# Splitting projected pieces of q and k on VectorE and GpSimd, in a graph attention kernel on one core

## The chip, the core and the metric

The kernel runs on one core of a Trainium2 chip. A core has TensorE (PE, matrix products; PEld in the profile is its loading of weights), VectorE (DVE), ScalarE (ACT), GpSimd (POOL) and SyncE (SP, which here issues all DMAs). They run their own streams of instructions, each in order, and wait for one another by semaphores. The metric is the device time of one execution in microseconds (us); the time before is a median of three runs.

## What is computed

Two layers over N = 2708 nodes with D = 128 features and a dense matrix adj, 2708 x 2708. The first is an attention in which adj is added twice to the scores; almost all of the work is there.

```python
# layer 0
q = (x @ Wq.T).reshape(d, n, h)      # d = 128, n = 2708, h = 8
k = (x @ Wk.T).reshape(d, n, h)
v = (x @ Wv.T).reshape(d, n, h)
a = einsum('dnh,dmh->dnm', q, k) * d ** -0.5 + adj + adj
a = softmax(a, axis=2)
out = einsum('dnm,dmh->dnh', a, v).reshape(n, h * d) @ Wo.T
x = layernorm(x + out)
# layer 1: two products with adj, and a second layernorm
hid = adj @ (x @ W2) + b2
x = layernorm(x + adj @ (hid @ W4) + b4 + hid @ res_w.T + res_b)
```

The reshape makes 128 independent attentions ("d"), each over 2708 queries and 2708 keys with 8 numbers per query and key: 128 x 2708 x 2708, some 940 million exponentials.

## The kernel before

**Scores.** With q scaled by half of D ** -0.5, exp(2 (q k + adj)) is the weight. The 128 attentions go in 32 groups of four (GB), the queries in six blocks of 452 (QB; the last has 448), the keys in 21 chunks of 128 and a short one of 20. q and k are each kept as two float32r numbers, a rounded part and what is left over, so that a score is one product with 32 rows of q and k per attention, four attentions side by side in PE.

**Two ways to a weight.** For most chunks, DVE adds adj to two scores at a time (L417, from PSUM into a tile `e`), and ACT takes exp of up to eight at once (L512). For nine of the chunks (TWO_EXP), ACT takes exp of three bare scores (L509, from the PSUM tile `p` into a tile `w`) and POOL multiplies them by exp(2 adj) (L510). The tiles exp(2 adj), `ecol`, are made by ACT in group 0 (L398), stored to DRAM, and loaded from there in all later groups (L298). The weights are multiplied with v and summed up in PSUM by PE (`add_up`, L427 to L435). DVE copies the sums of a block out (`hand_on`, L441), and SP stores them (L443).

**Steps.** A block is nine steps, one for each chunk of TWO_EXP: two to four "pieces" (pairs of scores) that DVE adds, three scores for POOL, and one exponential of each kind. There are 32 x 6 x 9 = 1728 steps, 54 to a group. ACT's work in a step is L509 and then L512.

**The order on PE.** The function `interleave` plans ahead in what order PE gets scores ("piece"), sums ("add_up"), copies ("hand_on") and projections ("amid"). It keeps an account of times (`pe`, `act`, `pool`, and `added`, the times at which DVE's adds end) with constants such as PRODUCT (a sum over a chunk), PROJECT and SPLIT, and gives PE next what it expects to be ready. A score needs one of two PSUM buffers (tag `s`), which comes free when DVE has added from it; a projection takes one of the same buffers.

**Projections amid the loop.** The first 256 of x's rows are projected ahead of the loop, two chunks of 128 (FIRST) by three weights. They suffice for group 0. The other 20 chunks are projected within it, as 120 "pieces of projection" (`halves`: chunk, one of k, q and v, half of the 1024 columns), each a product of 128x128 by 128x512 (L349). Two v pieces follow four of k and q. The list `amid` gives the step ahead of which each stands. `project` gives the product to PE, and DVE takes it from PSUM. For a v piece that is one copy (L352). For a q or k piece `split` reads PSUM twice, for the rounded part (L330) and for what is left over (L331), and then reduces the rounded part to its largest magnitude in `ends` (L332). The store, two DMAs for a q or k piece (L358), is put off to the next step, after its second piece, and waits there on SP. `load_half` loads the weights for the next piece.

**Bounds.** After the first layer the kernel looks whether its exponentials stayed in a safe range, and runs a slower attention with maxima if not. The largest q and k in `ends` are part of that.

**Other work in a group's steps.** SP loads adj (L295, L302) and exp(2 adj) (L298) eight tiles ahead, the next group's keys in steps 0 to 31 and the next block's q. POOL orders the next group's keys (L261) in steps 33 to 49 and spreads its values (L278, L279) in steps 50 to 53.

Of the kernel before, what the change touches and what calls it, by code (L numbers as in the profile page):

```python
# [9 lines left out]
F32 = mybir.dt.float32  # L10
# [8 lines left out]
P = 128  # L19
H = 8  # L20
GB = 4
NB = 512
# [5 lines left out]
SUM_HIGH = 1e30  # L28


QK_LIMIT = 7.5
EPS = 1e-5


# [4 lines left out]
def interleave(plan, blocks, short, amid=(), bufs=4, patience=0.1):  # L39

    SCORES, SAME_ROWS, AFTER_SHORT, SHOWN, PRODUCT, SHORT_PRODUCT, AGAIN, ADD, OVERLAP, COPY, MULTIPLY, HOP = (
        0.40, 0.2, 0.31, 0.15, 0.89, 0.96, 0.80, 1.04, 0.03, 0.56, 3.1, 0.12)
    EXP, EXP_ADDED, EXP_TILE = 0.07, 0.14, 0.37
    PROJECT, SPLIT = 0.95, 1.75  # L50
    n_plan = len(plan)
    users = [{m for p in pieces for m, _ in p} | {two} for pieces, two, _ in plan]
    held = {}
    for i, (pieces, two, _) in enumerate(plan):
        for p in pieces:
            for m, _ in p:
                held.setdefault(m, set()).add((False, i))
        held.setdefault(two, set()).add((True, i))
    complete = [[m for m in sorted(held, key=lambda m: (m != short, m)) if max(i for _, i in held[m]) == k] for k in range(n_plan)]
    first_chunk, last_chunk = ends_of(plan, short)  # L60
    pe = act = pool = banks = free_acc = 0.0
    added = [-1.0, -1.0]
    ready, summed, queue, sums, again = {}, {}, [], None, False
    n, c, left = 0, 0, None
    amid, seen = set(amid), 0
    while n < blocks * n_plan or queue:
        starts = []
        if n in amid and c == 0 and seen < n:
            starts.append((added[-2] + HOP, "amid"))
        elif n < blocks * n_plan:  # L70
            (b, i), (ob, oi) = divmod(n, n_plan), divmod(n - bufs, n_plan)
            pieces, two, batches = plan[i]
            left = list(batches) if left is None else left
            tiles = pieces[c]
            old = [summed.get((ob, x)) for x in users[oi]] if n >= bufs else [0.0]
            if None not in old:
                at = added[-2] + HOP
                rows = [r for m, j in tiles for r in (range(GB) if m == short else [j])]
                beside = [j for j in left if j not in rows][:2] if banks + HOP <= max(pe, at) else []
                if c == len(pieces) - 1:  # L80
                    beside = list(left)
                    at = max(at, banks + HOP) if left else at
                starts.append((at, "piece"))
        if queue and not (queue[0][1] == first_chunk and sums is not None):
            qb, qm = queue[0]
            at = max([ready[p, qb * n_plan + k] for p, k in held[qm]] + [free_acc] * (qm == first_chunk)) + HOP
            starts.append((at, "add_up"))
        soon = [s for s in starts if s[0] <= pe + patience]
        at, what = soon[0] if soon else min(starts)
        pe = max(pe, at)  # L90
        if what == "add_up":
            queue.pop(0)
            pe += SHORT_PRODUCT if qm == short else AGAIN if again else PRODUCT
            again = True
            summed[qb, qm] = pe
            yield "add_up", qb, qm, None
            if qm == last_chunk:
                sums = qb, pe
            continue
        again = False  # L100
        if what == "amid":
            pe += PROJECT
            added.append(max(added[-1], pe + SHOWN) + SPLIT)
            seen = n
# [36 lines left out]
def graph_attention_gcn(ctx: ExitStack, tc: tile.TileContext, x, xT, adj, adjT, adjP, adjS,  # L141
# [39 lines left out]
    near_exp = {(b, m): dram.tile([P, QB], F32, name=f"ne{b}_{m}") for b in range(len(QBS)) for m in TWO_EXP}  # L181


    ends = const.tile([P, 2, 2 * NM], F32, name="ends")
    nc.gpsimd.memset(ends, 0.0)


    with ExitStack() as s:
# [135 lines left out]
            t = t.rearrange("p a b -> p (a b)")  # L324
            return t if n == 1 else t.rearrange("p (n w) -> p n w", n=n)

        def split(o, src, i, end, mul=nc.vector.tensor_scalar_mul):

            f = half_scale if i == 1 else 1.0
            mul(o[:, 0].bitcast(F32R), src, f)  # L330
            nc.vector.scalar_tensor_tensor(o[:, 1].bitcast(F32R), src, f, o[:, 0], ALU.mult, ALU.subtract)  # L331
            nc.vector.tensor_reduce(end, o[:, 0], AX.X, ALU.max, apply_absolute_value=True)  # L332

        def load_half(n):
            c, i, h = halves[n]
            i0, mi = MC[c]
# [6 lines left out]
        def project(n):  # L343

            c, i, h = halves[n]
            i0, mi = MC[c]
            dst = projections[i][1]
            pp = ps.tile([P, 2, NB], F32, tag="s", name="s")
            nc.tensor.matmul(pp[:mi, 0, :], given[c][:, :mi], given.pop((c, i, h)), start=True, stop=True)  # L349
            o = proj.tile([P, 2, NB], F32, tag="pr", name="pr")  # L350
            if i == 2:
                nc.vector.tensor_copy(o[:mi, 0], pp[:mi, 0])  # L352
                return lambda: nc.sync.dma_start(dst.rearrange("(i g) e -> i (g e)", g=P)[ds(i0, mi), ts(h, NB)], o[:mi, 0])
            split(o[:mi], pp[:mi, 0], i, ends[:mi, i, ds(2 * c + h, 1)])

            def store():
                for l in range(2):
                    nc.sync.dma_start(dst.rearrange("r (i g) -> i r g", g=P)[ds(i0, mi), ds(H * l + 4 * h, 4)],  # L358
                                      o[:mi, l].rearrange("p (e g) -> p e g", g=P))
            return store  # L360

        first_x = flat(ppool.tile([P, 3, QB], F32, tag="w", name="w"))
        nc.sync.dma_start(first_x[:, : FIRST * P], xT[:, : FIRST * P])
# [6 lines left out]
        for i, (_, dst) in enumerate(projections):  # L370
            for c in range(FIRST):
# [5 lines left out]
                    nc.scalar.copy(o[:, 0], flat(pp))  # L377
                    nc.sync.dma_start(dst.rearrange("(i g) e -> i (g e)", g=P)[ts(c, P)], o[:, 0])
                else:
                    split(o, flat(pp), i, ends[:, i, 2 * c : 2 * c + 1], nc.scalar.mul)  # L380
                    nc.sync.dma_start(dst.rearrange("r (i g) -> i r g", g=P)[ts(c, P)],
                                      o.rearrange("p l (e g) -> p (l e) g", g=P))
            if i == 1:
# [10 lines left out]
        def first_exp(b, m):  # L394

            nw = QBS[b][1]
            t = ecols.tile([P, QB], F32, tag="ecol", name="ecol")
            nc.scalar.activation(t[:, :nw], adj_cols[0, b, -1 - m][:, :nw], AF.Exp, scale=2.0)  # L398
            nc.sync.dma_start(near_exp[b, m][:, :nw], t[:, :nw])
            exp_cols[0, b, m] = t  # L400

        def score(to, g, b, m, j):
            nw = QBS[b][1]
# [40 lines left out]

        where = {}

        amid = list(range(2, 54, 6))
        amid += range(56, 56 + 13 * (len(halves) - len(amid)), 13)
        for g in range(1, NG):
            c = (min(NG, g + 2) * GB * N - 1) // (P * P)  # L450
            assert c < FIRST or amid[halves.index((c, 2, 1))] + 8 < 54 * g
        stores = []
        loaded = ahead
        for what, n, c, beside in interleave(plan, len(steps) // len(plan), NU, amid):
            if what == "amid":
                at = amid.index(n)
                stores.append(project(at))
                if at + 1 < len(halves):
                    load_half(at + 1)
                continue  # L460
# [7 lines left out]
            g, b, i = steps[n]  # L468
            pieces, two, _ = plan[i]
            nw = QBS[b][1]  # L470
            if c == 1 and stores:
                stores.pop()()
            if c == 0:
                nq = (g, b + 1) if b + 1 < len(QBS) else (g + 1, 0)
                if i == 3 and nq[0] < NG:
# [30 lines left out]
            add_near(e, st, g, b, pieces[c], at)  # L506
            at += 2
            if c == len(pieces) - 1:
                nc.scalar.activation(w[:, :, :nw], sp[:, :, :nw], AF.Exp, scale=2.0)  # L509
                nc.gpsimd.tensor_mul(w[:, :, :nw], w[:, :, :nw],  # L510
                                     exp_cols[g, b, two][:, :nw].unsqueeze(1).to_broadcast([P, 3, nw]))
# [42 lines left out]
    def layer0_out(sb, ps, pa, judge):  # L554
# [72 lines left out]
        if judge:  # L627
# [1 line left out]
            nc.vector.tensor_scalar(finite, ys.rearrange("p c f -> p (c f)"), 0.0, 0.0, ALU.mult, ALU.is_equal)  # L629
            nc.vector.tensor_reduce(fine[:, 0:1], finite, AX.X, ALU.min)  # L630
            bounds = [(reach[:, 0, :], ALU.min, SUM_LOW, ALU.is_ge), (reach[:, 1, :], ALU.max, SUM_HIGH, ALU.is_le)]
            for i in range(2):
                limit = QK_LIMIT * (1.0, half_scale)[i]
                bounds.append((ends[:, i, :], ALU.max, limit, ALU.is_le))
# [195 lines left out]
```

## Time and profile before

| | |
|---|---|
| median of three runs | 6994.23 us (6991.26 to 6994.96) |
| the profiled execution | 7000.04 us, its span 6998.3 us |
| ahead of the loop | to 46.9 us |
| the loop, 32 groups | from 46.9 us to some 6658 us |
| group 0 (nine pieces of projection) | 235.2 us |
| groups 1 to 27 (111 pieces, three to five in a group) | 202.6 to 209.0 us each |
| groups 28 to 30 (no piece; nor has 31) | 200.1 us each |
| the rest (out of the first layer, second layer) | some 340 us |

A group's time is read from the start of POOL's first multiplication (L510) in one group to that in the next.

The costliest groups of instructions, with the count, the time that they were busy and the mean of one:

| line, engine | what | count | busy us | mean ns |
|---|---|---|---|---|
| L510 POOL | w times exp(2 adj), 128x1356 | 1728 | 5349.2 | 3101 |
| L417 DVE | scores plus adj, 128x904 | 5568 | 5889.6 | 1092 |
| L512 ACT | exp of e | 1728 | 4625.9 | 2677 |
| L509 ACT | exp of p | 1728 | 2312.3 | 1338 |
| L349 PE | projection, 128x512 | 240 | 134.2 | 641 |
| L330, L331, L332 DVE | split of a q or k piece | 80 each | 55.3, 55.3, 54.0 | 691, 691, 675 |
| L352 DVE | copy of a v piece | 40 | 27.6 | 691 |

In the profile, "idle before, releaser" names the time that an engine stood still ahead of an instruction and whose work ended that. In a timeline each line has the start and the duration in us, the engine, the line of the kernel, the operation, what is written and read, the shapes, and in brackets the idle time ahead of it. A line of a table by windows has the window, its length, the busy time of PE, PEld, DVE, ACT and POOL (with the number of instructions), the granted clock of PE, the share of the DMA engines that was busy, and GB/s. The end of a matmul is modelled, so PE's busy share is not a measure of what PE has left.

### The profile page before, as it was taken

Reading aid. Unit: us, or ns where it says so; the run is one execution under the profiler, and the core shown is the slowest. Engines: PE = TensorE matmul, PEld = TensorE weight load, DVE = VectorE, ACT = ScalarE, POOL = GpSimd, SP = SyncE. Lnnn points to the kernel's source line nnn. Section 1 sums busy time; section 2 is a strip of 40 time slices with the busy share of each in tenths; the row PEclk is TensorE's granted clock in tenths of the full one; section 3 lists DMA queues with packets and bytes.
Section 4 is the critical chain, followed back from the end, with each engine's and each line's share of the span. In section 5 each row is a group of like instructions: output and inputs, shape, how many; then the busy total and the mean of one; then the engine's idle time right before and its main releaser. Section 6 shows DMA issues by size and latency. Waiting matters only on the chain.

```text
span 6998.3 us, 137155 instructions
## 1 busy us (share of the span) xinstructions
PE 6733.7 (96%) x50426; PEld 2044.4 (29%) x50426; DVE 6186.2 (88%) x6363; ACT 6509.2 (93%) x3605; POOL 5624.8 (80%) x2387
## 2 busy tenths in 40 slices
PE   7999999999999999999999999999999999999979
PEld 2222222222222222222222222222222222222254
DVE  7899999999999999999999999999999999999941
ACT  7999999999999999999999999999999999999920
POOL 5888888888888888888888888888888888888800
PEclk8999999999999999999999999999999999999999
DMA  8877777777787777877777777877777777777667
GB/s 276 266 243 241 238 240 238 241 237 243 242 247 238 238 239 236 249 237 239 239 235 244 241 248 242 241 237 238 246 238 241 233 234 239 235 230 229 222 195 234
DMA packets 1143256, 1674.14 MB, mean 239 GB/s; under 512 B 148922, under 2 KB 1090366, under 8 KB 1138478
## 3 DMA queue, kind: packets, MB, share of 16 engines
q1 hardware_dynamic: 1142574, 1665.29, 77.0%
q8 instruction: 399, 6.54, 0.4%
q14 instruction: 283, 2.32, 0.1%
HBM read 1582.90 MB, written 81.80 MB: 238 GB/s over the span
## 4 chain that ended last, share of the span: by engine, by line
PE 49%; DMA 14%; DVE 12%; issue 8%; ACT 7%; SPq 5%; POOL 5%; DVEq 0%; ACTq 0%; POOLq 0%
PE acc L435 23%; PE s L410 16%; DVE e L417 10%; DMA col<-in_adjP 6%; POOL w L510 5%; ACT w L509 3%; ACT e L512 3%; PE acc L657 3%; DMA two<-in_adjP 3%; SPq L286 3%; DMA ecol<-ne 2%; PE p L410 2%; PE acc L427 2%; PE acc L432 1%; PE s L349 1%
## 5 line engine op out<-in xcount | busy, mean ns | idle before, releaser
L510 POOL TENSOR_TENSOR w<-w,ecol 128x1356 f32<-128x1356 f32 (+1 forms) x1728 | 5349.2, 3101 | 991.1 <-ACT w L509 864.0
L417 DVE TENSOR_TENSOR e<-s,col 128x904 f32<-128x904 f32 (+1 forms) x4608 | 4840.8, 1092 | 394.6 <-PE s L410 217.7
L512 ACT ACTIVATE e<-e 128x2712 f32<-128x2712 f32 (+5 forms) x1728 | 4625.9, 2677 | 61.1 <-DVE e L417 60.2
L435 PE MATMUL acc<-e,vals 128*9 128x452 f32 x20352 | 3564.6, 547 | 0.5 <-ACT e L512 0.2
L410 PE MATMUL s<-q,k 32*128 32x452 f32 x10944 | 2488.0, 464 | 134.8 <-DVE e L417 71.2
L509 ACT ACTIVATE w<-p 128x1356 f32<-128x1356 f32 (+1 forms) x1728 | 2312.3, 1338 | 94.4 <-PE p L410 54.2
L410 PEld LDWEIGHTS s<-q,k 32*128 32x128 f32 x10944 | 1032.3, 183 | 3320.4 <-DVE e L417 2817.3
L435 PE MATMUL acc<-w,vals 128*9 128x452 f32 x10368 | 1634.3, 548 | 0.0
L410 PE MATMUL p<-q,k 32*128 32x452 f32 (+1 forms) x5184 | 1282.5, 444 | 21.9 <-ACT w L509 20.9
L417 DVE TENSOR_TENSOR e<-s,two 128x904 f32<-128x904 f32 (+1 forms) x960 | 1048.8, 1093 | 91.2 <-PE s L410 34.1
L435 PEld LDWEIGHTS acc<-e,vals 128*9 128x9 f32 x20352 | 457.1, 89 | 818.4 <-issue 794.5
L410 PEld LDWEIGHTS p<-q,k 32*128 32x128 f32 x5184 | 529.6, 183 | 70.5 <-ACT w L509 55.4
L435 PEld LDWEIGHTS acc<-w,vals 128*9 128x9 f32 x10368 | 207.6, 89 | 217.4 <-issue 184.4
L261 POOL CAST k<-k_raw 128x336 fp32r<-128x336 f32 x251 | 222.4, 887 | 34.3 <-DMA q<-qs 34.3
L432 PE MATMUL acc<-e,v_first 128*32 128x452 f32 (+1 forms) x1536 | 188.3, 559 | 52.5 <-DVE o L441 46.3
L427 PE MATMUL acc<-e,v_short 128*128 128x452 f32 (+1 forms) x384 | 196.8, 594 | 0.0
L349 PE MATMUL s<-wc,xc 128*128 128x512 f32 (+1 forms) x240 | 134.2, 641 | 0.0
L441 DVE COPY o<-acc 128x452 f32<-128x452 f32 x192 | 118.7, 618 | 6.2 <-PE acc L435 6.2
L657 PE MATMUL acc<-col,xw 128*128 128x512 f32 (+2 forms) x264 | 105.8, 550 | 0.0
L657 PE MATMUL acc<-col,hw 128*128 128x512 f32 (+2 forms) x264 | 104.1, 545 | 0.0
L549 ACT ACTIVATE sd<-mv,eps 128x1 f32<-128x1 f32 (+1 forms) x22 | 5.9, 291 | 104.7 <-DVE mv L543 104.7
L669 ACT COPY hw<-ph 128x128 f32<-128x128 f32 (+1 forms) x22 | 5.4, 265 | 98.7 <-PE ph L668 98.6
(86 smaller groups left out, 1044.0 us busy)
## 6 DMA issues: line engine op xcount, KB each, us to landing
col<-in_adjP SPq DMA_DIRECT2D x1965, 226.0 KB
two<-in_adjP SPq DMA_DIRECT2D x1440, 226.0 KB
ecol<-ne SPq DMA_DIRECT2D x1395, 226.0 KB
col<-in_adjP SPq DMA_DIRECT2D x393, 224.0 KB
two<-in_adjP SPq DMA_DIRECT2D x288, 224.0 KB
ecol<-ne SPq DMA_DIRECT2D x279, 224.0 KB
col<-in_adjT SPq DMA_DIRECT2D x210, 256.0 KB
k_raw<-ks SPq DMA_DIRECT2D x512, 84.6 KB
```

Source lines behind the costliest of these rows:

```text
L261: copy(k[:, :, ts(i, n)], t[:, ts(i, n * NU)].rearrange("p (q c) -> p c q", c=NU))
L286: nc.sync.dma_start(q[ds(32 * j + 2 * H * i, 2 * H), :nw].bitcast(F32), qs[:, ds((GB * g + j) * N + n0, nw)])
L349: nc.tensor.matmul(pp[:mi, 0, :], given[c][:, :mi], given.pop((c, i, h)), start=True, stop=True)
L410: nc.tensor.matmul(to[:, :nw], k[r, m, :], q[r], start=True, stop=True)
L417: nc.vector.tensor_add(e[:, ds(at, 2), :nw], st[:, :, :nw], a)
L427: nc.tensor.matmul(a[:, :nw], vz, e[:, t, :nw], start=False, stop=False)
L432: nc.tensor.matmul(a[ds(32 * j, 32), :nw], v_first[g % 2][:, ds(32 * j, 32)], e[:, t, :nw], start=True, stop=False)
L435: nc.tensor.matmul(a[ds(32 * j, VW), :nw], v[:, m, ds(VW * j, VW)], e[:, t, :nw], start=False, stop=(m == last_chunk))
L509: nc.scalar.activation(w[:, :, :nw], sp[:, :, :nw], AF.Exp, scale=2.0)
L510: nc.gpsimd.tensor_mul(w[:, :, :nw], w[:, :, :nw], exp_cols[g, b, two][:, :nw].unsqueeze(1).to_broadcast([P, 3, nw]))
L512: nc.scalar.activation(e[:, :at, :nw], e[:, :at, :nw], AF.Exp, scale=2.0)
L657: nc.tensor.matmul(acc[:, :nw], src[:mw, m, :], t[:mw, :nw], start=(m == 0), stop=(last is None and m == NM - 1))
```

## The change

Four things change.

- `project`: DVE takes a q or k piece from PSUM in one pass, scaled, into a tile `pa` in SBUF. What used to be two more passes of DVE becomes two jobs for POOL: a copy that rounds to float32r, and a subtraction. The jobs and the store are given out one per step, each in the step's second piece: copy, subtraction and store of a q or k piece are queued in three steps one after the other. A v piece is one DVE pass and a store as before.
- The planner counts TAKE, 0.7, on DVE and SPLIT, 1.25, on POOL for a piece, in place of SPLIT, 1.75, on DVE.
- `amid`: after group 0 pieces stand at steps 2, 10, 18 and 26 of each group, instead of at every 13th step.
- The bounds on q and k go, with their reductions (also the four ahead of the loop). In their place `look_at_near` lets DVE reduce the tiles exp(2 adj) to their smallest (groups 0 to 3) and largest (groups 4 to 7). Each of the 54 tiles is looked at once for each, in one group of four by the index of its chunk.

```diff
-    PROJECT, SPLIT = 0.95, 1.75
+    PROJECT, TAKE, SPLIT = 0.95, 0.7, 1.25
...
         if what == "amid":
             pe += PROJECT
-            added.append(max(added[-1], pe + SHOWN) + SPLIT)
+            added.append(max(added[-1], pe + SHOWN) + TAKE)
+            pool += SPLIT
...
-        def split(o, src, i, end, mul=nc.vector.tensor_scalar_mul):
-
-            f = half_scale if i == 1 else 1.0
-            mul(o[:, 0].bitcast(F32R), src, f)
-            nc.vector.scalar_tensor_tensor(o[:, 1].bitcast(F32R), src, f, o[:, 0], ALU.mult, ALU.subtract)
-            nc.vector.tensor_reduce(end, o[:, 0], AX.X, ALU.max, apply_absolute_value=True)
...
             nc.tensor.matmul(pp[:mi, 0, :], given[c][:, :mi], given.pop((c, i, h)), start=True, stop=True)
-            o = proj.tile([P, 2, NB], F32, tag="pr", name="pr")
+            a = proj.tile([P, NB], F32, tag="pa", name="pa")[:mi]
+            nc.vector.tensor_scalar_mul(a, pp[:mi, 0], half_scale if i == 1 else 1.0)
             if i == 2:
-                nc.vector.tensor_copy(o[:mi, 0], pp[:mi, 0])
...
-            split(o[:mi], pp[:mi, 0], i, ends[:mi, i, ds(2 * c + h, 1)])
+            o = proj.tile([P, 2, NB], F32R, tag="pr", name="pr")[:mi]
...
-            return store
+            return [lambda: nc.gpsimd.tensor_copy(o[:, 0], a),
+                    lambda: nc.gpsimd.tensor_sub(o[:, 1], a, o[:, 0].bitcast(F32)), store]
...
+        def look_at_near(g, b, m):
+            x = TWO_EXP.index(m)
+            if g < 8 and g % 4 == x % 4:
+                nc.vector.tensor_reduce(ends[:, g // 4, ds(b * len(TWO_EXP) + x, 1)], exp_cols[g, b, m][:, : QBS[b][1]],
+                                        AX.X, (ALU.min, ALU.max)[g // 4])
...
-        amid = list(range(2, 54, 6))
-        amid += range(56, 56 + 13 * (len(halves) - len(amid)), 13)
+        amid = list(range(2, 54, 6)) + [54 * g + t for g in range(1, NG) for t in (2, 10, 18, 26)]
+        amid = amid[: len(halves)]
...
-                stores.append(project(at))
+                jobs += project(at)
...
-            if c == 1 and stores:
-                stores.pop()()
+            if c == 1 and jobs:
+                jobs.pop(0)()
...
             if c == len(pieces) - 1:
+                look_at_near(g, b, two)
                 nc.scalar.activation(w[:, :, :nw], sp[:, :, :nw], AF.Exp, scale=2.0)
```

More of the change, by code (lines that the diff above doesn't have):

```diff
@@ L28 @@
 SUM_HIGH = 1e30
-QK_LIMIT = 7.5
+NEAR_LOW = 1e-30
+NEAR_HIGH = 1e18
 EPS = 1e-5
@@ L181, in graph_attention_gcn @@
     near_exp = {(b, m): dram.tile([P, QB], F32, name=f"ne{b}_{m}") for b in range(len(QBS)) for m in TWO_EXP}
-    ends = const.tile([P, 2, 2 * NM], F32, name="ends")
-    nc.gpsimd.memset(ends, 0.0)
+    ends = const.tile([P, 2, len(QBS) * len(TWO_EXP)], F32, name="ends")
     with ExitStack() as s:
@@ L349, in project @@
             nc.tensor.matmul(pp[:mi, 0, :], given[c][:, :mi], given.pop((c, i, h)), start=True, stop=True)
-            o = proj.tile([P, 2, NB], F32, tag="pr", name="pr")
+            a = proj.tile([P, NB], F32, tag="pa", name="pa")[:mi]
+            nc.vector.tensor_scalar_mul(a, pp[:mi, 0], half_scale if i == 1 else 1.0)
             if i == 2:
-                nc.vector.tensor_copy(o[:mi, 0], pp[:mi, 0])
-                return lambda: nc.sync.dma_start(dst.rearrange("(i g) e -> i (g e)", g=P)[ds(i0, mi), ts(h, NB)], o[:mi, 0])
-            split(o[:mi], pp[:mi, 0], i, ends[:mi, i, ds(2 * c + h, 1)])
+                return [lambda: nc.sync.dma_start(dst.rearrange("(i g) e -> i (g e)", g=P)[ds(i0, mi), ts(h, NB)], a)]
+            o = proj.tile([P, 2, NB], F32R, tag="pr", name="pr")[:mi]
             def store():
@@ L358, in store @@
                     nc.sync.dma_start(dst.rearrange("r (i g) -> i r g", g=P)[ds(i0, mi), ds(H * l + 4 * h, 4)],
-                                      o[:mi, l].rearrange("p (e g) -> p e g", g=P))
-            return store
+                                      o[:, l].bitcast(F32).rearrange("p (e g) -> p e g", g=P))
+            return [lambda: nc.gpsimd.tensor_copy(o[:, 0], a),
+                    lambda: nc.gpsimd.tensor_sub(o[:, 1], a, o[:, 0].bitcast(F32)), store]
         first_x = flat(ppool.tile([P, 3, QB], F32, tag="w", name="w"))
@@ L379, in graph_attention_gcn @@
                 else:
-                    split(o, flat(pp), i, ends[:, i, 2 * c : 2 * c + 1], nc.scalar.mul)
+                    f = half_scale if i == 1 else 1.0
+                    nc.scalar.mul(o[:, 0].bitcast(F32R), flat(pp), f)
+                    nc.vector.scalar_tensor_tensor(o[:, 1].bitcast(F32R), flat(pp), f, o[:, 0], ALU.mult, ALU.subtract)
                     nc.sync.dma_start(dst.rearrange("r (i g) -> i r g", g=P)[ts(c, P)],
@@ L451, in graph_attention_gcn @@
             assert c < FIRST or amid[halves.index((c, 2, 1))] + 8 < 54 * g
-        stores = []
+        jobs = []
         loaded = ahead
@@ L631, in layer0_out @@
             bounds = [(reach[:, 0, :], ALU.min, SUM_LOW, ALU.is_ge), (reach[:, 1, :], ALU.max, SUM_HIGH, ALU.is_le)]
-            for i in range(2):
-                limit = QK_LIMIT * (1.0, half_scale)[i]
-                bounds.append((ends[:, i, :], ALU.max, limit, ALU.is_le))
+            bounds += [(ends[:, 0, :], ALU.min, NEAR_LOW, ALU.is_ge), (ends[:, 1, :], ALU.max, NEAR_HIGH, ALU.is_le)]
             for i, (a, way, limit, op) in enumerate(bounds):
```

## The prediction

> **What bounds the kernel now.** I read the page's busy times first, then the stages by windows, then the timelines of ACT and DVE around single pieces of projection.
>
> ```profile
> PE 6733.7 (96%) x50426; PEld 2044.4 (29%) x50426; DVE 6186.2 (88%) x6363; ACT 6509.2 (93%) x3605; POOL 5624.8 (80%) x2387
> ```
>
> Four engines are near full, so the average decides nothing. The windows (time, then busy time of each engine) compare two groups that hold no piece of projection (28 and 29) with two that hold eight (10 and 11):
>
> ```profile
> 6057.50:6457.70 400.20, 394.22 (x3064) 114.47 (x3060) 367.84 (x361) 400.20 (x217) 351.29 (x148) 1.00 0.76 234
> 2143.70:2557.80 414.10, 401.60 (x3068) 115.82 (x3060) 379.31 (x379) 402.21 (x217) 351.49 (x148) 0.99 0.78 239
> ```
>
> In the first row ACT is busy for all 400.20 us: without pieces the loop is bound by ACT, at 200.1 us for a group. In the second ACT does the same work and idles 11.9 us. So the floor under any change of the projections is ACT's 200.1 us per group. Groups 1 to 27 begin with POOL multiplications at 282.1 us and end at 5857.4 us: 5575.3 us for 27 groups, against 27 x 200.1 = 5402.7. The **172.6 us** between them is all that the 111 pieces in these groups cost, 1.55 us each, and all that can be won there. Group 0 (nine pieces) took 235.2 us; 200.1 plus ACT's 54 exponentials of 0.58 us (L398) is 231.5, so its pieces cost about 4 us.
>
> How ACT comes to idle is seen at two pieces ahead of the same kind of step (step 0 of the nine in a block). DVE at a q/k piece, three passes:
>
> ```profile
> 484.38 0.69 DVE L330 TENSOR_SCALAR pr<-s 128x512 fp32r<-128x512 f32 x1 [0.58 <-PE s L349]
> 485.10 0.69 DVE L331 SCALAR_TENSOR_TENSOR pr<-s,pr 128x512 fp32r<-128x512 f32 x1
> 485.71 0.67 DVE L332 TENSOR_REDUCE ends<-pr 128x1 f32<-128x512 f32 x1
> 486.30 4.15 DVE L417 TENSOR_TENSOR e<-s,col 128x904 f32<-128x904 f32 x4
> ```
>
> DVE at a v piece, one pass, with PE between its adds, and what ACT then waits:
>
> ```profile
> 933.18 0.69 DVE L352 COPY pr<-s 128x512 f32<-128x512 f32 x1 [0.57 <-PE s L349]
> 933.79 1.09 DVE L417 TENSOR_TENSOR e<-s,col 128x904 f32<-128x904 f32 x1
> ...
> 934.24 0.94 PE L435 MATMUL acc<-e,vals 128*9 128x452 f32 x8
> 935.11 0.48 PE L410 MATMUL s<-q,k 32*128 32x452 f32 x2
> ...
> 935.65 1.10 DVE L417 TENSOR_TENSOR e<-s,col 128x904 f32<-128x904 f32 x1 [0.77 <-PE s L410]
> ...
> 937.00 1.30 ACT L509 ACTIVATE w<-p 128x1356 f32<-128x1356 f32 x1 [0.61 <-PE p L410]
> ...
> 939.38 3.22 ACT L512 ACTIVATE e<-e 128x3616 f32<-128x3616 f32 x1 [1.08 <-DVE e L417]
> ```
>
> The v piece is already what every piece becomes for DVE: one pass. Yet ACT loses 0.61 + 1.08 us. The planner charged it with SPLIT, 1.75 us, and so put two products (L435, 0.94 us each) between the first and the second score of the step; DVE stands 0.77 us for the late score. **The order that PE was given costs as much as DVE's passes.**
>
> I took, from ACT's start times in the timeline, how much longer the 13 steps around each piece last than the same steps of groups 28 to 30: q/k pieces 1.6 us, v pieces 1.4 us. By the step of the block ahead of which the piece stands: step 1 0.65, step 2 0.91, step 3 0.79, step 4 1.1, step 8 1.13, step 6 1.8, step 0 2.07, step 7 2.3, step 5 3.4 us. The cause of the spread shows in the groups without pieces: the last add of a step ends 2.1 us before ACT wants it in step 1, but only 0.46, 0.32 and 0.29 us before in steps 0, 5 and 7.
>
> **The change, part by part.**
>
> *Places.* The 111 pieces went through all nine steps evenly (13 leaves 4 over 9). Now they stand at steps 2, 10, 18, 26 of a group, which are steps 2, 1, 0, 8 of a block: 28 x 0.91 + 28 x 0.65 + 28 x 2.07 + 27 x 1.13 = 132 us in place of 172.6. Places alone win 40 us. They come every 8 steps instead of 13; the loss lies in the step before a piece and the four after it, so 8 is enough.
>
> *DVE's passes and the plan.* A q/k piece loses L331 and L332, 0.69 + 0.68 = 1.37 us of DVE; TAKE costs 0.69 by the rows L330 and L352. The plan's charge falls from 1.75 to 0.7 us, and the new order has one product fewer between the first scores after a piece, for v pieces too: 0.94 us. One of the two (1.37 or 0.94) held up each piece, so I take 1.1 us off each: steps 2 and 1 fall to 0, step 0 to 0.97, step 8 to 0.03: 28 us in all. No class in this trace costs nothing (the cheapest, v ahead of step 1, costs 0.57), and PE still spends 1.02 us on each piece (L349), so I leave 0.2 us for each of 111, 22 us. Sum 50 us instead of 172.6: **-123 us**. Ends: 0 off (132 us stay, -40) to all gone (-173).
>
> *POOL's two jobs.* 73 q/k pieces outside group 0 bring a copy and a subtraction. The subtraction, 512 elements at L510's 3101 ns for 1356: 1.17 us. For the copy, L278 (168 elements, 0.28 us from start to start) gives 0.85 and L261 (a cast, 336 elements in strides, 887 ns) gives 1.35; I take 1.0. POOL spends 3.1 of 3.7 us per step, so 2.2 us over two steps make the multiplication about 1 us late, for two or three steps. PE uses its product on the average 2.0 (step 1) to 5.4 us after its end, 1.3 at the least. That lead is the cover: I charge 4 us in all; with the cover gone it would be 1 us x 73. POOL's ordering of keys (L261) lies in steps 33 to 49 of a group, away from the new places except in group 0.
>
> A rule speaks against giving this work to POOL: the Trainium skill, "Perfetto Trace Analysis", section Optimizing Scalar/DVE Operations, warns that POOL and DVE share a read port of SBUF, so moving work between them may not help. If it held here, each job could stand behind a DVE add of 1.09 us: 2.2 us more per piece, a delay of 3.2 us that passes the lead of 2.0 by 1.2, or 88 us for 73 pieces. The row: L510's 1728 multiplications took 3052 to 3175 ns beside a DVE that was 92% busy, so none was ever held for one add. DVE's adds and its take have a PSUM operand, and the look reads one. I take the row: 0.
>
> *The looks.* 108 reductions of 128x452 in groups 0 to 7. By L332 (675 ns for 512, 1210 for 1024) one takes 0.61 us. The planner does not know them. They are queued on DVE behind the last add of a step and ahead of the first add of the next, which PE's score buffers wait for. Group 0's 18 are covered by ACT's additional exponentials. Of the other 90 those ahead of steps with a lead over 0.6 us cost nothing; those ahead of steps 5, 7 and 0 (6, 12, 6 of them) cost 0.3, 0.3 and 0.15, and 24 ahead of steps 6 and 8 0.1 for what is left a step later: 1.8 + 3.6 + 0.9 + 2.4 = 9 us. Ends: 0 and, were all exposed, 90 x 0.61 = 55. A new wait: DVE now waits for the transfer of ecol, 0.5 to 2.4 us before POOL does. The tightest is step 5's, issued 6.8 us (median) before the look; POOL was found waiting for ecol 23 times in 1674, so I add nothing.
>
> *The stores.* The two DMAs of a q/k piece (0.395 us each on SP) move two steps later and wait for POOL's subtraction instead of DVE; behind them on SP stand the loads of the next step. When the subtraction ends DVE is in the middle of the store's step and these loads are used three steps later; the loads there were issued 7 to 16 us ahead so far. SP stands up to 9.2 us for each block's sums (L443, 966.7 us in all) without ACT idling in groups 28 to 31. Nothing.
>
> *Start and group 0.* Four reductions of 1.21 us leave the first projections: the second L331 starts at 12.22 behind one, about 0.5 us late. -1 us; group 0's pieces -2. The bounds at the end are as many as before: 0.
>
> Sum: -123 + 4 + 9 - 1 - 2 = -113. The profiled execution took 7000.0 us (span 6998.3); that gives 6887. The median of the runs is 5.8 lower: **6881 us**.
>
> **Rivals.**
> - *Only the places count* (0.22). The pieces keep their cost because it is PE's 1.02 us and DVE's 0.57 us wait for it, which stay. For it: v pieces cost only 0.2 less than q/k. Against it: the 0.77 us that DVE stands after a v piece is the second product, and it moves. -40 + 4 + 9 - 3 = -30: 6964.
> - *Nothing is left over* (0.07). The new places, eight steps apart, and the looks give the gain of the places back: 90 looks at 0.4 us instead of 0.1 add 27. -30 + 27: 6991, no change that can be told.
> - *POOL becomes the bound* (0.08): slower. The multiplication behind the two jobs comes later than PE needs it, PE stands in front of acc<-w (L435), and the scores queued behind it stand too. It decides where the delay passes the lead, that is above 1.3 to 2.0 us instead of the 1.0 I worked out: jobs of 3.2 us or more. Each piece then loses what the forecast gave it and up to 1 us more: -30 + 73 x 1.0 = +43: 7037. For it: POOL's 0.6 us of idle time per step. Against: the leads, and that POOL's key ordering puts 0.89 us on every second step in groups 28 to 30 while ACT stays full.
>
> The forecast has 0.63. Its own range, 20 to 90 us left of the 172.6, is 6850 to 6921. The range for 8 in 10 reaches to the places-only case: 6845 to 6966. A change within 0.2%, 14 us, can't be told from none. Faster: the forecast and the places case, 0.85; same 0.07; slower 0.08.
>
> **What would show it.** ACT busy above 99% in groups 8 to 27, these at 200.5 to 202.5 us instead of 206.5; groups 1 to 7 about 1 us longer than those; no 0.77 us hole between the first two adds after a piece; POOL's two jobs together near 2.2 us; waits of PE for POOL's product not above 28.3 us by more than a few; pieces ahead of step 0 still the dearest. The prediction is wrong if groups with pieces stay above 204 us, if PE waits for POOL, or if the looks cost DVE over 0.3 us each.

## The result, and the profile after

The changed kernel took 6971.26 us (median of six runs, 6961.13 to 6986.59) against 6995.19 us for the kernel before (six runs). The ratio is 0.9965, with a 95% interval of 0.995 to 0.9979: 24 us faster, where 113 were forecast, and outside the forecast's range. Measured again on another chip the ratio was 0.995 (0.9937 to 0.9962). The profile of the changed kernel is that of its longest execution, 6986.59 us; the profile of the second measurement (6970.4 us) is set beside it where it matters. From here on kernels are compared by their ratio to the kernel before on the same chip, since chips differ by some us; 0.001 is 7 us.

The page's busy times of the changed kernel:

```profile
PE 6734.9 (96%) x50426; PEld 2008.4 (29%) x50426; DVE 6129.9 (88%) x6307; ACT 6518.0 (93%) x3605; POOL 5761.0 (82%) x2546
```

DVE lost 56 us and POOL gained 136, as the change intends, and ACT idles in all only some 22 us less than before. The windows of the changed kernel show where (groups 10 and 11, with pieces; group 29, without; groups 8 to 27 together):

```profile
2150.40:2557.40 407.00, 399.40 (x3080) 114.19 (x3076) 372.93 (x369) 402.36 (x217) 359.87 (x159) 1.00 0.79 243
6043.20:6243.40 200.20, 196.91 (x1531) 56.57 (x1530) 183.28 (x180) 200.20 (x110) 175.64 (x74) 1.00 0.77 233
1735.70:5840.90 4105.20, 4005.51 (x30768) 1142.00 (x30760) 3730.93 (x3681) 4026.60 (x2161) 3606.29 (x1589) 1.00 0.79 241
```

Group 29 is at ACT's floor still. Groups 10 and 11 went from 414.1 to 407.0 us. Over groups 8 to 27 ACT's idle time (the window less ACT's busy time) is 78.6 us; it was 104.7 in the same groups before. Those twenty groups took 205.3 us each on the average, but six of them (8, 14, 15, 17, 23 and 24) 206.2 to 210.8, and it is in these that the granted clock fell, each time near step 23 (in group 24 near step 15 too). All six have a q or k piece ahead of step 18. The fourteen groups with such a piece there took 206.2 us each, the six with a v piece there (10, 13, 16, 19, 22 and 25) 203.1 (in the second measurement 205.1 and 203.5); before the change there was no such difference (206.2 and 206.8). Here is what DVE does there, at step 24 of group 8:

```profile
1821.28 2.10 DVE L422 TENSOR_TENSOR e<-s,col 128x904 f32<-128x904 f32 x2
1827.90 1.10 DVE L422 TENSOR_TENSOR e<-s,two 128x904 f32<-128x904 f32 x1 [4.52 <-DMA two<-in_adjP]
```

It stands for 4.52 us, waiting for a tile of adj, the double tile for step 6 of the block. The DMA queue of SP just before, in the same kernel:

```profile
1811.14 1.92 SPq L352 DMA_DIRECT2D qs<-pr  x2
1813.74 2.44 SPq L448 DMA_DIRECT2D os<-o  x4
1816.47 5.45 SPq L287 DMA_DIRECT2D q<-qs  x8
1821.96 0.42 SPq L299 DMA_DIRECT2D ecol<-ne  x1
1822.43 0.43 SPq L296 DMA_DIRECT2D two<-in_adjS  x1
1822.90 0.43 SPq L296 DMA_DIRECT2D two<-in_adjP  x1
```

The tile is asked for at 1822.4 and 1822.9 us, when DVE is ready for it at 1823.4. In front of it SP issued the store of the q piece (L352, the one that the change puts off by two steps), the block's sums and eight loads of q. The same place in the kernel before, without a store:

```profile
1805.75 1.39 SPq L443 DMA_DIRECT2D os<-o  x4
1807.24 4.26 SPq L286 DMA_DIRECT2D q<-qs  x8
1811.59 0.37 SPq L298 DMA_DIRECT2D ecol<-ne  x1
1812.00 0.43 SPq L295 DMA_DIRECT2D two<-in_adjS  x1
1812.47 0.43 SPq L295 DMA_DIRECT2D two<-in_adjP  x1
```

The sums and the loads of q took 7.9 us of SP in the changed kernel and 5.7 before, though they are the same twelve DMAs. The program gives its DMAs eight semaphores in turn, and SP issues a DMA when the eighth before it has landed: in all but one of SP's 1715 waits for a landing in the changed kernel it was the eighth before that it waited for. So the store also holds up what comes after it: here the third and fourth loads of q waited 0.90 and 0.34 us for its two halves to land.

The clock follows, in windows of the changed kernel around it (the granted clock is the third number from the end):

```profile
1818.00:1823.00 5.00, 4.94 (x37) 1.45 (x29) 4.82 (x6) 5.00 (x3) 4.56 (x2) 1.00 0.22 47
1823.00:1826.40 3.40, 1.95 (x13) 0.49 (x13) 0.38 (x1) 3.40 (x3) 2.80 (x2) 1.00 0.96 283
1826.40:1833.20 6.80, 4.15 (x21) 0.83 (x21) 4.13 (x4) 4.40 (x3) 3.22 (x2) 0.50 1.02 287
1833.20:1840.00 6.80, 6.80 (x52) 1.71 (x48) 5.61 (x7) 4.23 (x3) 4.05 (x2) 0.99 1.05 306
```

PE runs dry, and for 6.8 us it is granted half its clock, so that with this one late tile ACT idles 5.0 of the 17 us from 1823 to 1840. Nothing like the first wait was in the forecast.

### The profile page after: what moved, and what is told of

It reads as the page before. It is cut to its first block, busy times and chain, and to the rows that moved or that the text cites. A ratio compares the mean times of both kernels' runs of the same rounds, so it can differ in the third digit from the quotient of the medians.

```text
span 6984.8 us, 137327 instructions
## 1 busy us (share of the span) xinstructions
PE 6734.9 (96%) x50426; PEld 2008.4 (29%) x50426; DVE 6129.9 (88%) x6307; ACT 6518.0 (93%) x3605; POOL 5761.0 (82%) x2546
## 4 chain that ended last, share of the span: by engine, by line
PE 48%; DMA 15%; DVE 12%; ACT 9%; issue 7%; SPq 5%; POOL 4%; DVEq 0%; ACTq 0%; POOLq 0%
PE acc L440 22%; PE s L415 16%; DVE e L422 10%; DMA col<-in_adjP 8%; ACT e L518 5%; POOL w L516 4%; ACT w L515 4%; PE acc L661 3%; DMA two<-in_adjP 2%; SPq L287 2%; PE acc L432 2%; PE p L415 2%; DMA ecol<-ne 2%; PE acc L437 1%; PE s L343 1%
## 5 line engine op out<-in xcount | busy, mean ns | idle before, releaser
L516 POOL TENSOR_TENSOR w<-w,ecol 128x1356 f32<-128x1356 f32 (+1 forms) x1728 | 5347.8, 3101 | 840.5 <-ACT w L515 740.9
L415 PEld LDWEIGHTS s<-q,k 32*128 32x128 f32 x10944 | 1016.3, 182 | 3414.6 <-DVE e L422 2974.0
L415 PE MATMUL p<-q,k 32*128 32x452 f32 (+1 forms) x5184 | 1334.6, 443 | 5.0 <-ACT w L515 4.4
L440 PEld LDWEIGHTS acc<-e,vals 128*9 128x9 f32 x20352 | 443.0, 88 | 782.1 <-issue 778.5
L415 PEld LDWEIGHTS p<-q,k 32*128 32x128 f32 x5184 | 546.1, 183 | 43.3 <-ACT w L515 29.5
L345 DVE TENSOR_SCALAR pa<-s 128x512 f32<-128x512 f32 (+1 forms) x120 | 82.8, 690 | 52.5 <-PE s L343 51.8
L555 ACT ACTIVATE sd<-mv,eps 128x1 f32<-128x1 f32 (+1 forms) x22 | 5.9, 291 | 104.7 <-DVE mv L549 104.7
```

Of the source, the lines that this page charges most:

```text
L415: nc.tensor.matmul(to[:, :nw], k[r, m, :], q[r], start=True, stop=True)
L440: nc.tensor.matmul(a[ds(32 * j, VW), :nw], v[:, m, ds(VW * j, VW)], e[:, t, :nw], start=False, stop=(m == last_chunk))
L516: nc.gpsimd.tensor_mul(w[:, :, :nw], w[:, :, :nw], exp_cols[g, b, two][:, :nw].unsqueeze(1).to_broadcast([P, 3, nw]))
```

## The experiments

Numbers "by step" are taken as in the prediction: from ACT's start times, how much longer the steps around a piece last than the same steps of groups without one, in groups 8 and later. Single steps are given without the pieces at which the clock was halved; averages include them unless it is said. They are good to about 0.1 us.

**The places alone.** The kernel before, with only the list `amid` changed.

```diff
-        amid = list(range(2, 54, 6))
-        amid += range(56, 56 + 13 * (len(halves) - len(amid)), 13)
+        amid = list(range(2, 54, 6)) + [54 * g + t for g in range(1, NG) for t in (2, 10, 18, 26)]
+        amid = amid[: len(halves)]
```

> The kernel before with the new places alone (steps 2, 10, 18, 26 of a group); VectorE still makes all three passes, and the stores still wait for VectorE in the piece's own step. If the places are worth what the table by step of the block gave (132 instead of 172.6 us), 6955 us. If the whole of the measured gain of 24 us is that of the places and the rest of the change is worth nothing, 6971. If eight steps are too few to recover, 6985 or more.

Ratio 0.9966 (0.9952 to 0.998): as much as the whole change. In its profile groups 1 to 28 (the last three of the 111 pieces now stand in group 28) lost 148 us to pieces, against 173 before and 132 by the table: the places are worth more than nothing, but only some 25 us of the 40. Pieces ahead of step 1 cost 1.2 us here, where the table had 0.65. Whether that comes of standing every eight steps was not tried. No tile was late: DVE waited 6.9 us for double tiles in all, against 6.4 before, so the new places do no harm while the store goes out in the piece's own step.

**The old places.** The changed kernel with `amid` of before: the same edit the other way.

> The changed kernel with the places of before (every 13th step). If the places make the gain, it is lost: 6995 to 7011. If the passes and the plan make it, 6971 or less. The pieces then stand ahead of all nine steps, which gives a table of the new scheme by step of the block to set beside that of before.

Ratio 0.9897 (0.988 to 0.9913): 72 us faster than before, and faster than the changed kernel. The new places, good for the old scheme, are bad for the new one. A piece cost 0.83 us on the average of groups 8 to 27 (before: 1.54, or 1.32 without the pieces at which the clock was halved). By step: 0 0.85, 1 0.6 to 0.9, 2 0.5, 3 0.7, 4 0.27, 5 1.05, 6 0.9, 7 1.2 to 1.3, 8 1.25. DVE's waits for double tiles were those of before (6.5 us), and the clock was never halved in groups 1 to 28.

**The stores put off.** The changed kernel; stores of q and k pieces wait, from group 1 on, for step 5 or 6 of a block.

```diff
-            if c == 1 and jobs:
+            if c == 1 and jobs and (g == 0 or jobs[0].__name__ != "store" or i in (5, 6)):
```

> The changed kernel with the stores of q and k pieces put off, in groups 1 and later, to the next step 5 of a block (or 6), behind the loads that steps 6 and 7 need. Theory of the late load: the store that waits for GpSimd's subtraction holds SP just ahead of the load of the double tile for step 6, VectorE stands for it up to 4.5 us and the clock of TensorE halves afterwards; then some 2 us per group go, 6915 to 6935, and VectorE's waits for that tile fall from 29.6 us to under 10. Rival, that the pieces cost TensorE and the plan what they cost: 6971, with no change in groups 8 to 27.

Ratio 0.9901 (0.9885 to 0.9918). Groups 8 to 27 fell from 205.3 to 203.4 us each. The waits for the tile fell from 29.6 to 16.3 us, not under 10; the longest from 4.5 to 1.8. The usual margin in the third block did not grow (median from the end of the tile's issue to its use 4.1 us, 4.25 in the changed kernel); it is the latest tiles that are gone. From the first of the sums to the tile SP still takes 7.5 us there (median; 6.2 before), since it waits for the landings of other loads, of adj above all; why these land late was not found.

**The loads of q put off.** The changed kernel, compared on the same chip with itself.

```diff
-                if i == 3 and nq[0] < NG:
+                if i == 5 and nq[0] < NG:
                     load_q(*nq)
```

> The changed kernel once more, on the same chip as the three beside it, to be compared with them: a ratio of 0.9965, as measured, within 0.995 to 0.998.

> The changed kernel with nothing moved but the eight loads of the next block's q on SP: asked for at step 5 of a block in place of step 3. Theory of the late load: SP's own issuing (5.45 us for the eight) stands between the wait for GpSimd's subtraction and the load of the double tile for step 6; then that tile comes some 5 us earlier, VectorE's waits for it fall from 29.6 us to under 10, and the ratio is 0.990 as with the stores put off. If the wait for the subtraction itself is what makes it late, the ratio stays near 0.9965.

Ratio 0.9888 (0.9873 to 0.9903), beside 0.995 (0.9937 to 0.9962) for the changed kernel. DVE's waits for double tiles (time in all, times, longest), first in the changed kernel, at its first measurement and at the one on this chip, and then with q put off:

```profile
DVE e L422 <- DMA two<-in_adjP: 29.6, 36, 4.5
```

```profile
DVE e L422 <- DMA two<-in_adjP: 23.0, 33, 2.5
```

```profile
DVE e L422 <- DMA two<-in_adjP: 3.3, 14, 0.2
```

The groups with a q or k piece and those with a v piece ahead of step 18 now take the same, 202.8 us. DVE waits a little for q instead (9.4 us in all, 0.6 at the longest).

This run alone does not say whether SP's wait for POOL's subtraction made the tile late, since the room that the loads of q leave would cover such a wait too. The profiles do. In the changed kernel SP was found waiting for the subtraction 23 times, 16.0 us in all, but 12.4 us of these lie in the fourth block of a group; ahead of the store in the third block it is some 3.5 us in groups 1 to 27, and under 0.7 us in the six groups that were long. With the old places SP waited 70.0 us for it, up to 5.3 at a time, without loss. What made the tile late is what stands ahead of it: in the third block of a group the store came directly in front of the sums, q and this tile, with the tile due some 6 us after it is asked for even without a store (median in that block before: 6.2 us from the end of its issue to its use; changed kernel: 4.25; with q put off: 7.45). Two ways of shortening that piece of SP's queue give some 43 us.

**The passes alone.** The changed kernel with the old places and the plan's old charge.

```diff
-    PROJECT, TAKE, SPLIT = 0.95, 0.7, 1.25
+    PROJECT, SPLIT = 0.95, 1.75
...
-            added.append(max(added[-1], pe + SHOWN) + TAKE)
-            pool += SPLIT
+            added.append(max(added[-1], pe + SHOWN) + SPLIT)
```

> The changed kernel with the old places and the plan's old charge for a piece (1.75 us on VectorE, nothing on GpSimd): of the passes taken from VectorE alone. If the plan's order is worth as much as the passes, pieces cost some 1.3 us and the ratio is 0.995. If the passes alone do it, 0.990 as with the new plan. If the order alone does it, 0.998 or more.

Ratio 1.0014 (1.0007 to 1.002): slower than before. Some 12 us of that are the looks (below), which this kernel has too. In groups 8 to 27, which have no look, the profiles give 206.2 us each, against 206.4 before: the work that was taken from DVE bought some 4 us there without the plan's two numbers. With them these groups take 203.5. The halved clock goes with the charge as well: 13 stretches in groups 1 to 28 before, 13 here, none with the new charge. Which of the two numbers does it, and what the new charge would do for q and k pieces that DVE still splits, was not tried. The lines of DVE and of ACT at a q or k piece ahead of step 0 of group 10, under the old plan:

```profile
2293.40 0.69 DVE L344 TENSOR_SCALAR pa<-s 128x512 f32<-128x512 f32 x1 [0.57 <-PE s L342]
2294.01 1.09 DVE L421 TENSOR_TENSOR e<-s,col 128x904 f32<-128x904 f32 x1
2295.87 1.10 DVE L421 TENSOR_TENSOR e<-s,col 128x904 f32<-128x904 f32 x1 [0.78 <-PE s L414]
...
2297.22 1.30 ACT L514 ACTIVATE w<-p 128x1356 f32<-128x1356 f32 x1 [0.79 <-PE p L414]
2299.61 3.22 ACT L517 ACTIVATE e<-e 128x3616 f32<-128x3616 f32 x1 [1.08 <-DVE e L421]
```

And the same piece with the new charge (the kernel with the old places):

```profile
2252.11 0.69 DVE L345 TENSOR_SCALAR pa<-s 128x512 f32<-128x512 f32 x1 [0.57 <-PE s L343]
2252.72 2.20 DVE L422 TENSOR_TENSOR e<-s,col 128x904 f32<-128x904 f32 x2
2255.09 2.10 DVE L422 TENSOR_TENSOR e<-s,col 128x904 f32<-128x904 f32 x2 [0.17 <-PE s L415]
...
2255.18 1.34 ACT L515 ACTIVATE w<-p 128x1356 f32<-128x1356 f32 x1
2257.28 3.22 ACT L518 ACTIVATE e<-e 128x3616 f32<-128x3616 f32 x1 [0.77 <-DVE e L422]
```

Both have one pass of 0.69 us. Under the old charge DVE has its pass done and then stands 0.78 us for a score that PE was told to make late; under the new one two adds follow at once, the first of ACT's two holes is gone and the second is smaller.

**An honest charge for v pieces, in the kernel before.** No work changes.

```diff
-            added.append(max(added[-1], pe + SHOWN) + SPLIT)
+            added.append(max(added[-1], pe + SHOWN) + (TAKE if order.index(n) // 2 % 3 == 2 else SPLIT))
```

> The kernel before with one number of the plan changed: a v piece is charged with the 0.7 us that VectorE really spends on it, q and k pieces with 1.75 as before. No work changes. If the order was what made v pieces dear (the prediction's reading of the 0.77 us hole), the v pieces fall from 1.4 us by some 0.7 and the kernel gains 38 x 0.7 = 27 us, a ratio of 0.996. If it was TensorE's own time and the wait for it, nothing: 1.000.

Ratio 0.9971 (0.9961 to 0.9982), 20 us for one number where 27 were named. By step the v pieces fell from 1.90 to 0.81 (step 0), 1.03 to 0.25 (step 4), 1.57 to 0.88 (step 6) and 2.32 to 1.29 (step 7); q and k pieces stayed, but for those ahead of step 8 (1.16 to 1.9). The fallen values are those of q and k pieces in the kernel with the old places.

**The product made twice.** The changed kernel with the old places; each product of a piece is made a second time into the same place, and the plan is told 1.9 us.

```diff
             nc.tensor.matmul(pp[:mi, 0, :], given[c][:, :mi], given[c, i, h], start=True, stop=True)
+            nc.tensor.matmul(pp[:mi, 0, :], given[c][:, :mi], given.pop((c, i, h)), start=True, stop=True)
```

> The changed kernel with the old places and every projected piece's product made twice into the same place (the second overwrites the first), with 1.9 us for it in the plan. If TensorE's own time is what is left of a piece's cost (0.83 us on the average), each piece costs another 0.95 us: 0.990 plus 111 x 0.95 = 105 us, a ratio of 1.005. If the lead of VectorE over ScalarE covers it, 0.990 to 0.995.

Ratio 1.0046 (1.0033 to 1.0059), or 104 us more than with the product made once: 0.94 us for each of the 111 pieces. The profiles of the two kernels give 0.84 (93 us more in groups 1 to 28). So nearly all of what is added to PE's time comes back, at every step of the block (0.6 to 1.0 us). What is left of a piece's cost is on the average of the size of PE's own time for it; that it is that time is likely, but a piece ahead of step 4 costs only 0.27.

**All pieces ahead of step 4.** The changed kernel with `(4, 13, 22, 31)` in place of `(2, 10, 18, 26)`.

> The changed kernel with places 4, 13, 22 and 31 of a group, all of them ahead of step 4 of a block. With the old places a piece ahead of step 4 cost 0.27 us in groups 8 and later, against 0.8 on the average. If the cost is a matter of the step alone: 1.1 us per group in place of 3.4, 27 x 2.3 = 62 us below the old places' 0.990, so 0.981. If crowding (every 9 steps, stores in steps 6) brings the late load back, 0.990 or more.

Ratio 0.9879 (0.9863 to 0.9896), better than the old places' 0.9897 but with overlapping intervals, and not the 0.981 that the step alone would give. A piece cost 0.67 us there, not 0.27. Why the same step is dearer when pieces come every nine steps was not found; it was not late tiles (DVE waited 2.7 us for double tiles in all).

**The looks.** First the changed kernel without them (the array for their results is filled with 1, so that the bounds check nothing of exp(2 adj)).

> The changed kernel without the looks at exp(2 adj) (its bounds on these are left out). The prediction charged them with 9 us: 6962. Groups 1 to 7 of the changed kernel are some 3 us longer than groups 8 to 27: if that is the looks, 20 us, 6951. If the looks are covered, 6971.

Ratio 0.9912 (0.9896 to 0.9929), below all three that were named. Groups 1 to 7, where the looks are, took 204.9 us each against 207.5 in the profile of the changed kernel and 206.2 in that of its second measurement: 9 to 18 us. The whole time fell by more (26 to 37 us by the two measurements of the changed kernel), but part of that lies in groups 8 to 27, which have no look, and in which late tiles vary from run to run. With the old places, where no tile is late, groups 1 to 7 took 1.74 us more each than groups 8 to 27: 12 us. In two others without a halved clock, those with q put off and with all pieces ahead of step 4, it is 19 and 17 us.

Then the kernel with the old places, with the looks told to the plan.

```diff
-        free = added[-1] - OVERLAP
+        free = added[-1] - OVERLAP + look
+        look = 0.0
...
         if c == len(pieces):
+            g = n // n_plan // 6
+            look = LOOK if g < 8 and g % 4 == i % 4 else 0.0
```

> The changed kernel with the old places, and with the looks told to the plan (0.55 us of VectorE behind the last add of their step). Groups 1 to 7 of the same kernel without that (the old places alone) took 1.7 us more each than groups 8 to 27, 12 us in all. If an unplanned look is dear because TensorE then waits in a wrong order, half or more of it goes: 6 us or more, 0.989 or less against the kernel before. If VectorE's 0.61 us are the cost themselves, no difference: 0.990.

Ratio 0.9899 (0.9882 to 0.9915), against 0.9897. The interval holds 0.989 too; the profiles show no gain (groups 1 to 7: 205.3 us each, against 205.2).

Last, all pieces ahead of step 4 with the looks spread over all groups.

```diff
-            if g < 8 and g % 4 == x % 4:
-                nc.vector.tensor_reduce(ends[:, g // 4, ds(
+            if g % 16 == (4 * b + 7 * x) % 16:
+                nc.vector.tensor_reduce(ends[:, g // 16, ds(
...
```

> All pieces ahead of step 4 (0.988 when tried with the looks in groups 0 to 7), and the same 108 looks spread over all 32 groups, some three to a group in place of 12 to 18. If looks are dear because they crowd and eat up VectorE's lead, half of their 17 us goes: 0.9865. If each costs by itself, 0.988.

Ratio 0.9871 (0.9857 to 0.9886), an interval that holds both 0.9865 and 0.988. The profiles tell more: groups 1 to 7 gained 1.7 us each, groups 8 to 27 lost 0.6; over groups 1 to 27 the time above ACT's floor was 86.6 us, and 87.3 with the looks crowded. A look costs the same, crowded or spread. This is nevertheless the fastest kernel measured here, with the same work and bounds as the changed one: its interval lies below the changed kernel's, and overlaps those with q put off and with the looks crowded. All pieces ahead of step 4 together with q put off was not tried.

## Why the prediction was wrong, step by step

**The floor** held: 200.1 us per group without pieces, before and after, and ACT full there.

**Places, -40.** Alone, -24 (0.9966, that is -34 to -14). Right in kind, over-sized: 148 us were left in the profile and not 132, so that "8 is enough" is not borne out.

**Passes and plan, -83 beyond the places.** This is the first term that failed. The prediction saw that PE's order costs as much as DVE's passes. It is more than that: the passes without the plan's charge were worth next to nothing (206.2 us against 206.4 in groups 8 to 27), and the charge on top of them 82 us (1.0014 to 0.9897). The size failed in "One of the two (1.37 or 0.94) held up each piece, so I take 1.1 us off each", which let pieces at two of the four steps fall to zero, with 0.2 us left "for PE". At the old places 0.83 us are left, so 0.7 and not 1.1 us fall away, and part of the 0.7 is the halved clock. At the new places, with q put off and no tile late, a piece costs 0.68 us in groups 8 to 27, where the forecast has 50 us / 111 = 0.45: ahead of steps 0 and 8 no more than forecast (0.85 and 0.2, against 1.17 and 0.23), but ahead of steps 2 and 1, which were to fall to zero and keep 0.2, 0.97 and 0.70. To let these fall to zero is to take DVE's lead over ACT, 0.3 to 2.1 us, as cover for PE's time. The doubled product says that it is none for more of PE's time; that PE has no idle time afterwards in which to win the lead back is the likely reason, but was not measured.

**The stores, "Nothing".** The second term that failed, and the reason that the result is 24 and not some 69 to 78 us. The prediction asked whether SP's wait for POOL was harmful, correctly found that it was not, and took the loads behind the store to be "issued 7 to 16 us ahead". That reading was wrong in the trace of before already: it left out the double tile for step 6, used 6 us after its issue (4.6 at the least in the third blocks of groups 8 to 27). And it missed that two steps later the store of the third block's piece comes in front of it. Stores or q put off: 0.9901 and 0.9888 in place of 0.9965 and 0.995, some 43 us.

The two terms and the looks close the sum: with q put off the gain is 78 us, 35 short of 113; 26 of these are the 0.68 us per piece in place of 0.45, and some 10 the looks. The rest of the miss, up to the measured 24 to 35 us, is the late tile.

**POOL's two jobs, +4.** Right in mechanism. Rows of the changed kernel:

```profile
L357 POOL TENSOR_TENSOR pr<-pa,pr 128x512 fp32r<-128x512 f32 (+1 forms) x80 | 103.5, 1293 | 0.0
L404 DVE TENSOR_REDUCE ends<-ecol 128x1 f32<-128x452 f32 (+1 forms) x108 | 66.1, 612 | 9.7 <-ACT ecol L397 9.7
L356 POOL CAST pr<-pa 128x512 fp32r<-128x512 f32 (+1 forms) x80 | 49.3, 616 | 0.0
```

1.29 + 0.62 = 1.91 us per piece against 2.2 in the sum. PE's waits for POOL's product, before and after:

```profile
PEld acc L435 <- POOL w L510: 28.3, 116, 0.4
```

```profile
PEld acc L440 <- POOL w L516: 31.1, 130, 0.3
```

The lead covered the jobs, and the rival in which POOL becomes the bound is out. The multiplication took 3101 ns as before, so the shared port that the Trainium skill warns of ("Perfetto Trace Analysis", Optimizing Scalar/DVE Operations) was not felt here.

**The looks, +9.** 612 ns each, as worked out; somewhat under-sized, 12 to 19 us in groups 1 to 7 of the kernels in which no clock was halved. Group 0's 18 can't be told: group 0 took 232 to 238 us in kernels whose group 0 is the same.

**The rivals.** "Only the places count" named 6964, near the measured time by luck: the plan is worth more than the places, and the new places then cost the new scheme a late tile. Nothing in the rivals had a load on SP in it. One sign of being wrong that the prediction named came: groups 8 to 27 took 205.3 us, above 204.

## What to carry to other kernels

An order that was planned with a cost holds an engine to that cost after the work has become cheaper: when work moves between engines, change the planner's number with it, and measure the two apart. Of an instruction that is put off in a queue, look not only at what it waits for but at what it now stands in front of, and at the smallest margin from issue to use among these, not at the usual one. And before a lead of one engine over another is counted as cover for an added cost, double that cost once: here each added us of TensorE came back as nearly one.

## What was not expected of the hardware

A late tile is paid for twice. PE stood still from about 1825 to 1829 us; from 1826.4 us the granted clock was 0.50, for 6.8 us, most of it after the tile had come. The kernel before has 13 such stretches of 3.4 or 6.8 us in groups 1 to 28, the changed one 11 (6 in its second profile), the changed one with old places and old charge 13, and the kernels with stores or q put off or with the old places alone 2, 0 and 0. In one execution all of them start at whole multiples of 3.41 us from one another. In the kernel before, 9 of the 13 are at pieces ahead of step 5 of a block. A piece with such a stretch cost 3.5 us there, and would have cost 2.0 by the others at the same steps: some 20 of the 173 us that the prediction put down to pieces are the clock.

The Trainium skill's page "TensorE: Matmul & The Clock Gate" (Part 1, The HAM clock gate) has the half clock after an idle window of about 3.4 us. The lengths here agree with multiples of that. The start does not: in the changed kernel PE had stood for 1.5 us when the clock fell, and in the kernel before, in the one looked at near 1787 us, PE stood for DVE only twice, by 0.76 and 0.54 us. The 3.4 us before that stretch, and the stretch:

```profile
1783.70:1787.10 3.40, 2.11 (x19) 0.87 (x19) 3.27 (x4) 3.40 (x2) 1.71 (x1) 1.00 1.06 306
1787.10:1790.50 3.40, 3.40 (x18) 0.41 (x10) 2.52 (x3) 2.97 (x2) 2.70 (x1) 0.50 1.12 362
```

PE was busy for 2.11 of 3.40 us, as it was for 1.95 in the window of the changed kernel shown above. Over all stretches in groups 1 to 28 it was busy, its ends being modelled, for 62 to 78% of the 3.4 us before them in the kernel before, and for 37 to 81% in the changed one. So here a PE that is partly idle lost its clock. It is not enough to explain when: other 3.4 us with PE busy for 63% passed without a stretch. With the old places it is the plan's old charge that brings them about: they went with it while DVE's work stayed the same. What sets off a single one was not found.
